# The first image's second band moves into the prelude as plain convolutions; the first batch's other work becomes one chain, one piece a turn

## The chip, the cores and the metric

The kernel runs on one core of one Trainium2 chip. The core has five engines with instruction queues of their own: TensorE (PE in the profile, its weight loads PEld), VectorE (DVE), ScalarE (ACT), GpSimd (POOL) and SyncE (SP, which here only issues transfers). Each executes its queue in the order written. The metric is the device time in microseconds; lower is better. The kernel before takes 8226.97 us, the median of 3 runs (8226.15 to 8232.14).

## The reference

The input is four images of 64 x 64 positions with 128 channels, in float32; an image is 4096 tokens. Two layers follow one another. What matters here, for each image:

```python
c1 = conv3x3(elu(x), W1) + b1              # 128 -> 128 channels
c2 = conv3x3(c1, W2) + b2                  # 128 -> 256 channels
a, b = split(c2);  c3 = a * sigmoid(b)
q, k, v = c3@Wq+bq, c3@Wk+bk, c3@Wv+bv     # 4, 4 and 16 wide, causal attention over 4096 tokens
x1 = x + c3 + tile(atten(q, k, v), 8) @ W3 + b3

y = layernorm(x1)                          # second layer
h = y + attention(y@wq, y@wk, y@wv) @ wo   # 16 heads of 8, all 4096 x 4096 scores, not causal
t = x1 + h + (silu(h@w1) * (h@w3)) @ w2
out = t + mixture(layernorm(t))            # 8 experts, the two best by a router
```

The second layer's attention is by far the largest part: 16 heads x 4096 x 4096 exponentials for each image.

## The kernel before, in words

**Units.** An image is cut into 8 *chunks* of 512 tokens (8 image rows) and into 4 *bands* of two chunks (16 rows). Bands 0 and 1 hold the chunks 0 to 3, bands 2 and 3 the chunks 4 to 7. A batch is one image.

**The main stream.** `stream` walks through a written plan of *segments*: for one image, one group of four heads and one chunk of queries, a range of key tiles of 128. Each key tile is one *step* (`attention_step`): four score matmuls into two PSUM tiles, two exponentials of 128 x 1024 on ACT, four value matmuls into `acc`. There are 1024 steps per image. Steps are written so that a step's values follow the scores of the two steps after it (`finish(2)`). Keys lie in `kx`, which has four places of a quarter of the tokens; `key_quarter` brings them, ahead of time where the segment that needs them is ready. A segment is ready when `second` of its image, the number of chunks whose second-layer operands are written, has reached `n`. For the first image the plan has three parts, with n = 2, 4 and 8: 64 steps over the first two chunks, 192 more when there are four, 768 more when there are eight. For later images n is 8.

**Other work as pieces.** Everything else is written as Python generators that yield after each *piece* (some 0.46 us of TensorE work). The list `fillers` holds them; after each step the main loop may call `insert`, which takes one piece from the first filler. While an image's operands are incomplete, the credit for this grows by 1.0 a step. If the stream isn't ready, every turn of the loop takes a piece and no step.

**The chain of one image.** `convolutions` makes ELU, layer 1 and layer 2 band by band. Most bands use the Winograd form (`winograd`): POOL builds `row_terms` and `col_terms`, TensorE does 16 products, and DVE combines them. `first_attention` makes chunk c's query, key and value terms, puts the causal steps (`first_step`, c + 1 of them) into the stream and gathers the result in `ready`. `second_operands` then folds W3, makes the layer norm, transposes, makes the second layer's queries, keys and values of a chunk and stores them to HBM (`d_q`, `d_k`, `d_v`), from where the steps load them.

**The prelude.** For the first image nothing is there to stream at the start. `run_alone` turns through five generators: the convolutions, the first attention, the second layer's operands (`second_operands_beside`), and two that transform the weights for Winograd (`fold_and_spread`, `spread_beside`). Band 0 is made by `first_band` as plain convolutions: its inner function `nine` adds nine products of 128 x 512 in one PSUM bank, for layer 1 and for each half of layer 2. The prelude ends when two chunks are complete and the three weight transforms are done; what is left of the generators goes into one filler, `together`, which takes pieces from them in turn. Until four chunks are complete, the main loop takes two pieces a turn. Later images have no `together`: their `first_attention` draws on its `convolutions` and calls `second_operands` itself, one chain.

**One order for each engine.** `InOrder` records every instruction as depending on the one before it on its engine, so a queue is exactly in the order written; every instruction carries the line of that helper, L105, and the profile is read by tile names: `s` and `e` are scores and exponentials, `qx`, `kx`, `vg` the attention's operands, `m` the PSUM bank of the pieces (one buffer), `e_band` and `c_band` the padded bands before layer 1 and layer 2 (two each), `taps` the untransformed weights (`r` holds the third set).

Of the kernel before, what the change touches and what calls it, by code (L numbers as in the profile page):

```python
# [9 lines left out]
FP = mybir.dt.float32  # L10
FR = mybir.dt.float32r
AF = mybir.ActivationFunctionType
ALU = mybir.AluOpType
AX = mybir.AxisListType

P = 128
C = 128
IMG = 64
N = IMG * IMG
NT = N // P  # L20
QB = 512
# [94 lines left out]
def fast_path(ctx: ExitStack, tc: tile.TileContext, a: dict, where: dict, out: bass.AP, verdict):  # L116
# [33 lines left out]
    def chunk(tag, name=None):  # L150
        return wk.tile([P, QB], FP, tag=tag, bufs=CHUNKS.get(tag, 1), name=name or tag)
# [8 lines left out]
    alone = [True]  # L160
# [34 lines left out]
    taps1 = taps(a["L0_conv_W1"])  # L195
# [106 lines left out]
    def rows(ap):  # L302
        return ap.rearrange("p (h w) -> p h w", w=IMG)
# [34 lines left out]
    def row_terms(band):  # L338
        r = row_tile().rearrange("p (i y x) -> p i y x", i=4, y=8)
        for i, (x, y, op) in enumerate(SUMS):  # L340
            pool.tensor_tensor(r[:, i], band[:, x : x + 15 : 2, :], band[:, y : y + 15 : 2, :], op)
        return r
# [51 lines left out]
            late.pop(0)()  # L394
            yield 0.0, "free" if late else "stop"

    def first_band(st):


        def nine(taps, band, y, n):  # L400
            ps = rows(m_tile()[:, : n * IMG])
            for m in range(9):
                i, j = divmod(m, 3)
                pe.matmul(
                    ps,
                    lhsT=taps[:, i, j, :],
                    rhs=band[:, y + i : y + i + n, j : j + IMG],
                    start=m == 0,
                    stop=m == 8,
                )  # L410
                if m in (2, 5):
                    yield 0.0, "stop"
            return ps

        pool.memset(e_band[0][:, 0, :], 0.0)
        pool.memset(c_band[0][:, 0, :], 0.0)
        for band, y, n, to in (
            (e_band[0], 0, 8, slice(1, 9)),
            (e_band[0], 8, 8, slice(9, 17)),
            (e_band[1], 0, 1, slice(17, 18)),  # L420
        ):
            ps = yield from nine(taps1, band, y, n)
            act.activation(c_band[0][:, to, 1 : IMG + 1], ps, AF.Identity, bias=b1)
            yield 0.0, "stop"
        st.c3 = wk.tile([P, 2 * QB], FP, tag="c3", bufs=2, name="c3")
        for h in range(2):
            c3, gate = st.c3[:, h * QB : (h + 1) * QB], chunk("sd", "gate")
            ps = yield from nine(taps2a, c_band[0], 8 * h, 8)
            act.activation(rows(c3), ps, AF.Identity, bias=half_b2a, scale=0.5)
            yield 0.0, "stop"  # L430
            ps = yield from nine(taps2b, c_band[0], 8 * h, 8)
            act.activation(rows(gate), ps, AF.Tanh, bias=half_b2[:, 1:2], scale=0.5)
            dve.scalar_tensor_tensor(c3, gate, 1.0, c3, ALU.add, ALU.mult)
            st.done.append(c3)
            yield 0.0, "stop"

    def tiles(ap):

# [2 lines left out]
    def convolutions(b, st):  # L441
# [75 lines left out]
        jobs = [(0, 0), (0, 1), (0, 2), (1, 0), (0, 3), (1, 1), (1, 2), (1, 3)]  # L517
        yield from elu(3)
        if b == 0:
            yield from first_band(st)  # L520
            jobs = [(0, 1), (0, 2), (1, 1), (0, 3), (1, 2), (1, 3)]
            while len(spread_of) < 3:
                yield 0.0, "wait"
            yield from elu(5)
        else:
            pool.memset(e_band[0][:, 0, :], 0.0)
        r_ = row_terms(e_band[jobs[0][1]])
        v = [col_terms(r_, j) for j in COLS]
        yield 0.0, "stop"
        for n, (layer, r) in enumerate(jobs):  # L530
            ahead, terms = [], []
            at_once = False
            if n + 1 < len(jobs):
                layer_, r_next = jobs[n + 1]
                if layer_ == 0:
                    yield from elu(min(2 * r_next + 3, NQ))
                    if r_next == 3:
                        pool.memset(e_band[1][:, 17, :], 0.0)

                at_once = layer_ == 0 or layer == 1 or r_next + 1 < r  # L540
                if at_once:
                    terms.append(row_terms((c_band if layer_ else e_band)[r_next % 2]))

            def used(q):
                if at_once:
                    ahead.append(col_terms(terms[0], COLS[q]))

            if layer == 0:
                yield from winograd(wino1, slice(0, C), v, b1, used, first(r))
                here, above = c_band[r % 2], c_band[(r - 1) % 2]  # L550
                if r == 0:
                    pool.memset(here[:, 0, :], 0.0)
                else:
                    pool.tensor_copy(here[:, 0, :], above[:, 16, :])
                    pool.tensor_copy(above[:, 17, :], here[:, 1, :])
                if r == 3:
                    pool.memset(here[:, 17, :], 0.0)
            else:
                while b == 0 and len(st.ready) < 2 * r - 2:
                    yield 0.0, "wait"  # L560
                st.c3 = wk.tile([P, 2 * QB], FP, tag="c3", bufs=2, name="c3")
                yield from winograd(wino2, slice(0, C), v, half_b2a, lambda q: None, second(r, False))
                yield from winograd(wino2, slice(C, 2 * C), v, b2[:, 1:2], used, second(r, True))
                st.done += [st.c3[:, :QB], st.c3[:, QB:]]
                yield 0.0, "done"
            if n + 1 < len(jobs) and not at_once:
                terms.append(row_terms(c_band[r_next % 2]))
                ahead = [col_terms(terms[0], j) for j in COLS]
            v = ahead
# [8 lines left out]
    def first_attention(b, st):  # L578
# [3 lines left out]
        for c in range(NQ):  # L582
            while len(st.done) <= c:

                r = (0.0, "wait") if b == 0 else next(st.conv)
                if r[1] != "done":
                    yield r
            while b == 0 and st.second < c - 1:
                yield 0.0, "wait"
            c3 = st.done[c]  # L590
            t = xt
# [46 lines left out]
            dve.tensor_tensor(t, ps, t, ALU.add)  # L638
            yield 0.6, "stop"

            while b == 0 and st.read < c:
                yield 0.0, "wait"
            sums, found = [], []
            for r in range(c + 1):
# [1 line left out]
            while not found:  # L646
                yield 0.0, "rounds"
            st.ready.append((t, found[0]))
            while b > 0 and st.second <= c:
                yield from second_operands(b, st)  # L650
        dve.tensor_reduce(seen[:, 0, b : b + 1], top0.rearrange("p i c -> p (i c)"), AX.X, ALU.max)
        dve.tensor_reduce(seen[:, 1, b : b + 1], top_v0, AX.X, ALU.max)
# [87 lines left out]
    def second_operands_beside(b, st):  # L740

        while st.second < NQ:
            while len(st.ready) <= st.second or not folded[0]:
                yield 0.0, "wait"
            yield from second_operands(b, st)

# [293 lines left out]
    class Batch:  # L1040


        def __init__(self, b):

            dims = {
                "t": [NQ, P, QB],
                "h": [NQ, P, QB],
                "k": [P, 2, N],
                "q": [NQ, P, 2, 2, QB],
                "v": [NG1, P, NQ, 4 * NSLOT * (1 + HD1)],  # L1050
                "a": [NQ, NG1, P, QB],
                "r": [NQ, P, QB // HD1],
                "g": [NQ, P, P],
            }
            if b == 0:
                dims["p"] = [NG1, NQ, P, QB]
            self.d = {name: dram.tile(shape, FP, tag=name, name="d_" + name) for name, shape in dims.items()}
            self.done, self.ready, self.second, self.read = [], [], 0, 0
            self.conv = convolutions(b, self)
            scratch.append(self.d)  # L1060
            batches.append(self)

    batches = []

    def together(gens):

        gens = list(gens)
        while gens:
            for _ in range(len(gens)):
                r = next(gens[0], None)  # L1070
                while r is not None and r[1] in ("held", "rounds"):
                    yield r
                    r = next(gens[0], None)
                gen = gens.pop(0)
                if r is not None:
                    gens.append(gen)
                    if r[0] > 0.0:
                        yield r[0], "stop"
                        break
                if not gens:  # L1080
                    return
            else:
                yield 0.0, "stop"

    def run_alone(gens, until):

# [181 lines left out]
    def spread_beside():  # L1268
# [4 lines left out]
    st = batches[0]  # L1273
    left = run_alone(
        [st.conv, first_attention(0, st), second_operands_beside(0, st), fold_and_spread(), spread_beside()],
        lambda: st.second >= plan[0].n and len(spread_of) == 3,
    )
    alone[0] = False
    fillers.append([together(left), PREPARE, None, False])

    steps = stream()
    credit, waiting = 0.0, False
# [4 lines left out]
    while True:  # L1287
# [22 lines left out]
        free = bool(fillers) and fillers[0][3]  # L1310
        if waiting or not quiet[0] and (free or credit > 0.0 and (left >= PIECE or credit > 2.8)):
            took = insert()
            if b == 0 and batches[0].second < plan[0].n + 2:
                took += insert()
            credit -= took
            left -= took
        ahead = min(max(left, 0.0), AHEAD)
# [721 lines left out]
```

## Time and profile before

| | |
|---|---|
| median of 3 runs | 8226.97 us |
| profiled execution | 8229.92 us |
| its span in the trace | 8228.1 us |
| granted TensorE clock, mean | 0.988 |
| ACT busy, share of the span | 7866.6 us, 96% |
| PE busy, share of the span | 8022.1 us, 97% |
| DVE and POOL busy | 2459.5 and 681.1 us |
| exponentials of 128 x 1024 and their busy time | 8480, 7809.3 us |

The execution's time beside its span is what lies around the trace's first and last instruction. Busy time is counted once where instructions of one engine overlap, so one exponential takes 7809.3 / 8480 = 0.92 us of ACT, a step 1.84, although its own duration is given as 1112 ns. A window view gives the busy time of each engine between two moments, with the granted clock of TensorE. In a timeline the brackets name the idle time before an instruction and what ended it.

### The profile page before, as it was taken

How to read it: one execution, taken by the hardware profiler on the slowest of the kernel's cores; microseconds unless marked ns; L12 is line 12 of the kernel's file. 1: busy time of each engine (PE TensorE's matmuls, PEld its weight loads, DVE VectorE, ACT ScalarE, POOL GpSimd, SP SyncE). 2: the span in 40 equal slices, each digit the busy share in tenths (PEclk: the TensorE clock that was granted, in tenths of full speed). 3: DMA queues.
4: the chain of work that ended last, by engine and by line, in shares of the span. 5: the costliest groups of instructions: out<-in, count | busy, mean ns of one | idle time of the engine just before them, and what ended most of it. 6: DMA issues, size and time to landing. Idle time of an engine off the chain costs nothing.

```text
span 8228.1 us, 173041 instructions
## 1 busy us (share of the span) xinstructions
PE 8022.1 (97%) x73335; PEld 2481.8 (30%) x73335; DVE 2459.5 (30%) x5068; ACT 7866.6 (96%) x8679; POOL 681.1 (8%) x615
## 2 busy tenths in 40 slices
PE   6799999999999999999999999999999999999998
PEld 3222222222333332333333333222333333232233
DVE  5433122222332222333332223333333332121123
ACT  2499999999999999999999999999999999999996
POOL 3201101000000012110000002211000000000000
PEclk8899999999999999999999999999999999999999
DMA  2122010101110100011110000001111111111121
GB/s 70 52 67 76 24 42 30 51 27 45 49 34 17 39 22 26 34 38 49 38 36 24 27 27 28 28 30 48 35 48 45 47 47 52 37 37 42 58 68 33
DMA packets 213940, 334.24 MB, mean 41 GB/s; under 512 B 31555, under 2 KB 107811, under 8 KB 213155
## 3 DMA queue, kind: packets, MB, share of 16 engines
q1 hardware_dynamic: 209139, 321.31, 12.0%
q8 instruction: 577, 9.45, 0.5%
q10 hardware_dynamic: 4016, 1.77, 0.1%
q14 instruction: 208, 1.70, 0.1%
HBM read 195.09 MB, written 127.93 MB: 39 GB/s over the span
## 4 chain that ended last, share of the span: by engine, by line
PE 67%; issue 3%; ACT 1%; DVE 1%; POOL 0%; DMA 0%; ACTq 0%; DVEq 0%; POOLq 0%
PE acc L105 33%; PE s L105 22%; PE m L105 13%; ACT e L105 1%; DVE h L105 0%; POOL rs L105 0%; DVE added L105 0%; DVE at L105 0%; ACT neg L105 0%; POOL xt L105 0%; ACT t L105 0%; DVE by_e L105 0%; POOL v L105 0%; ACT th L105 0%; DMA d_r<-sums 0%
## 5 line engine op out<-in xcount | busy, mean ns | idle before, releaser
L105 ACT ACTIVATE e<-s 128x1024 f32<-128x1024 f32 x8480 | 7809.3, 1112 | 91.5 <-PE s L105 87.1
L105 PE MATMUL acc<-e,vg 128*9 128x512 f32 x32768 | 4333.7, 594 | 1.9 <-DVE at L105 1.9
L105 PE MATMUL s<-qx,f_kx 32*128 32x512 f32 (+1 forms) x16960 | 2909.2, 495 | 37.5 <-ACT e L105 27.7
L105 PEld LDWEIGHTS s<-qx,f_kx 32*128 32x128 f32 (+1 forms) x16960 | 1171.2, 181 | 4079.0 <-ACT e L105 3859.7
L105 PEld LDWEIGHTS acc<-e,vg 128*9 128x9 f32 x32768 | 715.9, 90 | 797.1 <-issue 463.7
L105 PE MATMUL m<-v,f_wino 128*32 128x256 f32 x5744 | 470.9, 405 | 54.9 <-DVE sd L105 16.8
L105 DVE TENSOR_TENSOR by_e<-m,gates 128x512 f32<-128x512 f32 x248 | 171.5, 691 | 736.9 <-PE m L105 733.9
L105 POOL TENSOR_TENSOR v<-r 128x1024 f32<-128x1024 f32 x120 | 232.6, 1945 | 1314.1 <-PE m L105 1313.6
L105 DVE COPY sd<-m 128x512 f32<-128x512 f32 x179 | 123.7, 691 | 673.6 <-PE m L105 673.6
L105 PE MATMUL m<-f_we,y2T 128*32 128x256 f32 x3968 | 316.9, 391 | 0.5 <-DVE by_e L105 0.5
L105 POOL TENSOR_TENSOR rs<-ve,f_minus_half 128x4 f32<-128x4 f32 x64 | 65.2, 1018 | 3029.2 <-DVE ve L105 3029.2
L105 DVE COPY at<-acc 128x512 f32<-128x512 f32 x130 | 89.9, 691 | 698.8 <-PE acc L105 696.4
L105 DVE TENSOR_REDUCE added<-by_e 128x128 f32<-128x1024 f32 x128 | 255.3, 1995 | 4.8 <-DMA d_g<-turned 0.5
L105 PE MATMUL m<-hT,f_fw 128*32 128x256 f32 (+1 forms) x2728 | 236.1, 391 | 0.0
L105 POOL TENSOR_TENSOR t<-t,h 128x512 f32<-128x512 f32 x32 | 41.0, 1281 | 2042.1 <-DVE h L105 2042.1
L105 DVE TENSOR_TENSOR t<-m,sums 128x256 f32<-128x256 f32 x135 | 57.3, 425 | 493.2 <-PE m L105 493.2
L105 PEld LDWEIGHTS m<-v,f_wino 128*32 128x32 f32 x5744 | 121.9, 111 | 247.2 <-issue 172.2
L105 DVE SCALAR_TENSOR_TENSOR h<-m,h 128x512 f32<-128x512 f32 (+1 forms) x93 | 64.2, 690 | 434.8 <-ACT th L105 276.3
L105 DVE TENSOR_TENSOR t<-m,t 128x512 f32<-128x512 f32 x62 | 42.9, 692 | 444.4 <-PE m L105 444.4
L105 DVE COPY h<-m 128x512 f32<-128x512 f32 (+1 forms) x93 | 64.2, 690 | 370.5 <-PE m L105 370.5
L105 PE MATMUL m<-e,f_v 128*32 128x512 f32 (+2 forms) x1128 | 149.7, 574 | 0.0
L105 DVE TENSOR_TENSOR e<-e,f_consts 128x128 f32<-128x128 f32 x128 | 29.1, 287 | 326.3 <-ACT e L105 326.3
(253 smaller groups left out, 3299.1 us busy)
## 6 DMA issues: line engine op xcount, KB each, us to landing
f_kx<-d_k SPq DMA_DIRECT2D x139, 512.0 KB
qx<-d_q SPq DMA_DIRECT2D x152, 256.0 KB
d_q<-two SPq DMA_DIRECT2D x64, 512.0 KB
d_a<-at SPq DMA_DIRECT2D x128, 256.0 KB
vg<-d_v SPq DMA_DIRECT2D x32, 576.0 KB
d_k<-two SPq DMA_DIRECT2D x32, 512.0 KB
d_v<-vc SPq DMA_DIRECT2D x32, 288.0 KB
xe<-in_x_dram SPq DMA_DIRECT2D x32, 256.0 KB
```

Of the source, the lines that this page charges most:

```text
L105: made = op(*args, **kw)
```

## The change

- `first_band` becomes `first_bands`: after band 0 it makes band 1 in the same way, with nine products for each bank, in the prelude. Ahead of it come the ELU pieces up to chunk 4 (the last row of layer 1 needs one row of the next band). Layer 1 is needed for the row above, which POOL copies from band 0.
- The prelude ends only when these two bands are done too (`st.plain`), beside the conditions of before.
- The Winograd jobs of the first image shrink from six to four, bands 2 and 3 in both layers, in the order (layer 1, band 2), (layer 1, band 3), (layer 2, band 2), (layer 2, band 3). Before, the order was layer 1 of bands 1 and 2, layer 2 of band 1, layer 1 of band 3, layer 2 of bands 2 and 3.
- `together` goes. After the prelude the generators become separate fillers, the second operands first, then the first attention. `second_operands_beside` returns at its first wait once the prelude is over, and the first attention then draws on the convolutions and calls `second_operands` itself. The waits of the first image that were bound to `b == 0` are bound to the prelude.
- The second piece a turn goes.

```diff
-    def first_band(st):
+    def first_bands(st, elu):
...
+        for r in range(2):
+            here, there = e_band[r], e_band[1 - r]
+            c_here = c_band[r]
+            if r == 0:
+                pool.memset(here[:, 0, :], 0.0)
+                pool.memset(c_here[:, 0, :], 0.0)
+            else:
+                yield from elu(5)
+                pool.tensor_copy(c_here[:, 0, :], c_band[0][:, 16, :])
+            for band, y, n, to in (
+                (here, 0, 8, slice(1, 9)),
+                (here, 8, 8, slice(9, 17)),
+                (there, 0, 1, slice(17, 18)),
+            ):
+                ps = yield from nine(taps1, band, y, n)
+                act.activation(c_here[:, to, 1 : IMG + 1], ps, AF.Identity, bias=b1)
+                yield 0.0, "stop"
+            st.c3 = wk.tile([P, 2 * QB], FP, tag="c3", bufs=2, name="c3")
+            for h in range(2):
...
+        st.plain = False
...
         if b == 0:
-            yield from first_band(st)
-            jobs = [(0, 1), (0, 2), (1, 1), (0, 3), (1, 2), (1, 3)]
+            yield from first_bands(st, elu)
+            jobs = [(0, 2), (0, 3), (1, 2), (1, 3)]
             while len(spread_of) < 3:
                 yield 0.0, "wait"
-            yield from elu(5)
+            yield from elu(7)
...
-                r = (0.0, "wait") if b == 0 else next(st.conv)
+                r = (0.0, "wait") if alone[0] else next(st.conv)
...
-            while b > 0 and st.second <= c:
+            while not alone[0] and st.second <= c:
                 yield from second_operands(b, st)
...
             while len(st.ready) <= st.second or not folded[0]:
+                if not alone[0]:
+                    return
                 yield 0.0, "wait"
...
-        lambda: st.second >= plan[0].n and len(spread_of) == 3,
+        lambda: st.second >= plan[0].n and len(spread_of) == 3 and not st.plain,
     )
     alone[0] = False
-    fillers.append([together(left), PREPARE, None, False])
+    fillers.extend([gen, PREPARE, None, False] for gen in reversed(left[1:]) if gen is not st.conv)
...
             took = insert()
-            if b == 0 and batches[0].second < plan[0].n + 2:
-                took += insert()
```

More of the change, by code (lines that the diff above doesn't have):

```diff
@@ L413, in nine @@
             return ps
[L415 to L435, printed above, removed]
+        for r in range(2):
[17 more added lines that the diff above has]
+            for h in range(2):
+                c3, gate = st.c3[:, h * QB : (h + 1) * QB], chunk("sd", "gate")
+                ps = yield from nine(taps2a, c_here, 8 * h, 8)
+                act.activation(rows(c3), ps, AF.Identity, bias=half_b2a, scale=0.5)
+                yield 0.0, "stop"
+                ps = yield from nine(taps2b, c_here, 8 * h, 8)
+                act.activation(rows(gate), ps, AF.Tanh, bias=half_b2[:, 1:2], scale=0.5)
+                dve.scalar_tensor_tensor(c3, gate, 1.0, c3, ALU.add, ALU.mult)
+                st.done.append(c3)
+                yield 0.0, "stop"
@@ L519, in convolutions @@
         if b == 0:
-            yield from first_band(st)
-            jobs = [(0, 1), (0, 2), (1, 1), (0, 3), (1, 2), (1, 3)]
+            yield from first_bands(st, elu)
+            jobs = [(0, 2), (0, 3), (1, 2), (1, 3)]
             while len(spread_of) < 3:
                 yield 0.0, "wait"
-            yield from elu(5)
+            yield from elu(7)
         else:
             pool.memset(e_band[0][:, 0, :], 0.0)
-        r_ = row_terms(e_band[jobs[0][1]])
+        r_ = row_terms(e_band[jobs[0][1] % 2])
         v = [col_terms(r_, j) for j in COLS]
@@ L558, in convolutions @@
             else:
-                while b == 0 and len(st.ready) < 2 * r - 2:
+                while alone[0] and len(st.ready) < 2 * r - 2:
                     yield 0.0, "wait"
@@ L583, in first_attention @@
             while len(st.done) <= c:
-                r = (0.0, "wait") if b == 0 else next(st.conv)
+                r = (0.0, "wait") if alone[0] else next(st.conv)
                 if r[1] != "done":
                     yield r
-            while b == 0 and st.second < c - 1:
+            while alone[0] and st.second < c - 1:
                 yield 0.0, "wait"
@@ L639, in first_attention @@
             yield 0.6, "stop"
-            while b == 0 and st.read < c:
+            while alone[0] and st.read < c:
                 yield 0.0, "wait"
@@ L1058, in __init__ @@
             self.done, self.ready, self.second, self.read = [], [], 0, 0
+            self.plain = b == 0
             self.conv = convolutions(b, self)
@@ L1063, in fast_path @@
     batches = []
[L1065 to L1083, printed above, removed]
     def run_alone(gens, until):
```

## The prediction

> **What bounds the kernel now.** I read the busy shares first, then a table of the span cut at the visible changes of pace. The Trainium skill ("Perfetto Trace Analysis", section "Identifying the Most-Contended Engine") says that occupancy is a fair measure for ScalarE and that busy matmul time isn't one for TensorE, so I follow ACT. The page:
>
> ```profile
> PE 8022.1 (97%) x73335; PEld 2481.8 (30%) x73335; DVE 2459.5 (30%) x5068; ACT 7866.6 (96%) x8679; POOL 681.1 (8%) x615
> ACT  2499999999999999999999999999999999999996
> ```
>
> The stages (window, its length, then busy us of each engine, PE clock, DMA share, GB/s):
>
> ```profile
> 0.00:153.50 153.50, 97.25 (x370) 48.50 (x370) 81.95 (x168) 15.57 (x22) 48.17 (x68) 0.84 0.28 82
> 153.50:326.00 172.50, 149.50 (x1479) 47.96 (x1480) 78.61 (x162) 134.49 (x145) 45.87 (x36) 0.99 0.12 35
> 326.00:412.80 86.80, 49.54 (x464) 19.23 (x464) 49.22 (x91) 0.76 (x2) 30.10 (x24) 0.55 0.23 80
> 412.80:750.00 337.20, 322.46 (x2880) 98.62 (x2880) 123.58 (x282) 319.94 (x352) 26.20 (x25) 0.96 0.23 74
> 750.00:1250.00 500.00, 496.00 (x4154) 144.59 (x4152) 120.53 (x238) 498.05 (x548) 78.58 (x63) 1.00 0.12 38
> 1250.00:8150.00 6900.00, 6867.62 (x63814) 2098.40 (x63810) 1972.85 (x4055) 6885.48 (x7600) 449.81 (x398) 1.00 0.12 38
> ```
>
> Length minus ACT busy is ACT's idle time: 137.9, 38.0, 86.0, 17.3, 1.9 and 14.5 us, then 65.8 in the tail. From 750 us on ACT never stops; the exponentials are the same number in both kernels. So the change is worth what it does to the 281.1 us of ACT idle before 1250. Stage 1 is the prelude. Stage 2 is the first 64 attention steps (142 exponentials: 128, and 14 of the first attention), stretched by two pieces a turn. Stage 3 is one wait, seen on ACT's timeline:
>
> ```profile
> 409.84 0.63 ACT L105 ACTIVATE t<-t 128x512 f32<-128x512 f32 x1 [83.71 <-DVE t L105]
> 412.85 1.02 ACT L105 ACTIVATE e<-s 128x1024 f32<-128x1024 f32 x1 [2.38 <-PE s L105]
> ```
>
> Step 65 belongs to a segment that needs chunks 2 and 3 (four ready). They come from band 1, whose Winograd convolution only starts at the end of the prelude; when the 64 steps run out, its second layer is still to do.
>
> **What the built order shows.** The instruction order of the changed program (not its time) settles what the diff leaves open. TensorE executes matmuls in program order; the skill says so ("TensorE: Matmul & The Clock Gate", section "Step-by-step: what each phase is for": only weight loads are pulled ahead), and a late operand in this trace does hold everything (7.04 us below). In the order, the second half of the key product of chunk 3 moves from the wait after step 64 to step 24; chunk 7's moves from step 199 to step 254. From step 1570 on the filler work stands where it stood.
>
> **Removed.** The 86.0 us wait at step 64 goes: chunk 3 is complete 40 steps (40 x 1.84 = 74 us) early. The double pieces of stage 2 go. A 4.9 us key-load wait inside stage 4, at the first use of the other two key places, goes too: with four chunks ready during the first segment, those places are loaded ahead.
>
> **Added: a longer prelude.** The first band shows what a plain band costs (PE timeline):
>
> ```profile
> 31.45 7.99 PE L105 MATMUL m<-f_e_band,taps 128*128 128x512 f32 x18 [0.78 <-ACT f_c_band L105]
> 40.23 2.22 PE L105 MATMUL m<-f_e_band,taps 128*128 128x64 f32 x18 [0.78 <-ACT f_c_band L105]
> 42.90 7.96 PE L105 MATMUL m<-f_c_band,taps 128*128 128x512 f32 x18 [0.45 <-issue]
> ```
>
> A nine takes some 7.8 us, and about 1 us to the next one for ACT to empty the bank. Following the new order:
> - Up to 88.6 (transposes of chunk 1) nothing moves. Then band 1's ELU pieces enter ahead of chunk 1's first attention. The vector queue (query terms, layer norm of chunk 0, key terms, ELU) lets the scores start about 99 instead of 90.3; chunk 1's sums are copied about 106.5 instead of 101.4. Band 1's first nine starts about 108.
> - First layer: 2 x 7.8 + 2.2 + 3 gaps of 1 = 21; pieces between: value and key products 1.24 + 1.03, W3 fold 2 x 0.6, one transpose 0.66. About 25, to 133.
> - Second layer: 4 x 7.8 + 4 gaps = 35; pieces between: wq1 1.1, values 1.24, keys 1.03, wq0 1.1 with its 1.3 wait, wk0/wv0 0.6, transpose 0.6, fold 0.6, three first steps 3 x (0.5 + 1.8) with 2.4 for ACT to free score banks. About 51, to 184.
> - Tail: the stream's first score stands behind chunk 3's query and key terms and chunk 2's layer norm on DVE (2.7 + 1.0 + 1.9 + 1.9 + 1.4 with POOL's power + 1.1), transposes 0.7, copy 0.9, half a product 0.6: 13 with latencies, to 197.
> - Clock: the skill (same page, section "Part 1: The HAM clock gate") puts the array at half rate until about 3.4 us of sustained work. The trace agrees: the first nine of all took 10.13 against 7.99. I add 2 there and 4 in the thin parts: **first exponential at 203**, 49.5 later.
>
> ACT busy within the prelude becomes 15.6 + 7 evacuations (4.5) + 6 exponentials moved here (5.6) = 25.7; idle 177.3, against 137.9: **+39.4**. The Winograd terms that POOL built there (about 19 us) go; they were off this path. The first key load has no late writer in front of it any more.
>
> **Steps 1 to 256.** One piece a turn. In stage 4, which already ran so, idle other than the 4.9 and 3.8 us DMA waits was 8.6 in 337 us; 2.5% of about 530 us (286 steps with the first attention's 30, at 1.84) is 13. To this: 3 for the start. 4 because one chain has no second piece to lie between dependent ones. At step 80 layer 2 of band 2 follows layer 1 of band 3 in the same chain, and POOL makes its row terms and first column term between; before, the other chain covered that place, but its like in the stall shows the price:
>
> ```profile
> 331.83 4.69 POOL L105 TENSOR_TENSOR r<-f_c_band 128x528 f32<-128x528 f32 x4
> 338.57 1.93 PE L105 MATMUL m<-v,f_wino 128*32 128x256 f32 x16 [7.04 <-POOL v L105]
> ```
>
> 7 less about 1 of scores in stock: 6. Nothing on PE can pass it, the next scores and values wait behind it.
>
> At step 257 comes the other cost: the segment needs all eight chunks; chunk 7's last product is issued in step 254, and the key load can't be issued before its write. The pair of transfers at the end of the old wait (SP, then PE):
>
> ```profile
> 403.36 0.54 SPq L105 DMA_DIRECT2D d_k<-two  x1
> 406.80 0.54 SPq L105 DMA_DIRECT2D f_kx<-d_k  x1
> 411.95 0.80 PE L105 MATMUL s<-qx,f_kx 32*128 32x512 f32 x4
> ```
>
> 8.6 us. After step 254's scores: product 0.95, DVE 2.0, transfers 8.6 = 11.6; three steps cover 5.5: **6**. The second batch's image loads stand ahead of the keys on SP (0.8 us each to issue), so up to 10. They replace the 3.8 wait that those loads caused in ACT's queue at 726 us. Sum for steps 1 to 256: 13 + 3 + 4 + 6 + 6 = **32**; and 6 for the rest to 1250 (1.9 before, with the second batch's preparation squeezed into 768 steps instead of 825).
>
> **Sum.** Idle 281.1 before; after 177.3 + 32 + 6 = 215.3: 65.8 less. ACT's work grows by 4.5 - 1.9 (one copy, two tanh) = 2.6. So 63 us less: span 8228.1 - 63 = 8165, execution 8167 (it read 8229.92). The median of the runs lies 3 us below that execution: **8164**, -0.77%.
>
> **Rivals.**
> - *Better, about 8138 (0.12).* The prelude ends at 192 as counted without a cold clock (-11), and steps 1 to 256 lose only 17 (-15). For it: band 0's nines kept clock 1.00 with the same gaps.
> - *A late step 257, 8184 (0.13).* Key load, values, queries and the second batch's image loads leave together, and one-chain waits cost 10 more: +20. For it: that prelude load took 11.3 us from the vector engine's last write to the first score. Against: little else moves then (74 GB/s in stage 4).
> - *Cold prelude, about 8206 (0.08).* At the 0.57 to 0.64 clock that the old prelude shows from 100 to 150, the 54 wide matmuls (46 us) take some 42 more. Against: old PE was idle half of that time; now it is nearly packed. At 0.55 in the old wait there were gaps behind every 1.9 us piece, here behind 8 us.
> - *Slower, about 8247 (0.04).* Removing the alternation of chains makes each piece wait on DVE for the one before it, and in-order PE passes the wait to ACT. The order has 170 turns with a piece in steps 1 to 256, of which I charge 17 us (0.10 each). It decides from (17 + 63)/170 = 0.47 us each; at stage 2's 38.0 / 64 = 0.59, 100 us, and 20 us over the old time. Against: between two pieces lie scores and values (about 1.4 us), more than the 0.7 copy that frees the bank; later batches run one chain with hardly any idle, though at lower density.
> - *The change doesn't take hold (0.02).* Step 65 still waits as long: 8164 + 86 = 8250. Only transfers 40 steps late could bring it; the order speaks against it.
>
> **Numbers.** The likeliest has 0.61, by itself 8150 to 8180. Range 8138 to 8204: it takes in the better case, the late step and nearly the cold one. A measurement of this kernel can tell about 0.2% (16 us). Faster needs below 8210.5: 0.61 + 0.12 + 0.13 + 0.06 of the cold case = 0.92; within 0.2% lies the rest of that, 0.02; slower are the last two, 0.06.
>
> **What would show it.** First exponential of the stream at 198 to 208. No ACT gap over 10 us after it. Step 64 done about 130 us after it (68 steps with the first attention's four). One gap near step 80, ended on POOL's column terms, and one of 4 to 10 us near 765, ended by keys. ACT idle to the end of step 256 near 210. Wrong if the prelude runs past 225, or if small PE waits on DVE add up to over 60 us in steps 1 to 256.

## The result, and the profile after

The changed kernel takes 8155.07 us (median; 8154.1 to 8159.66), beside 8229.15 us for the kernel before in the same session: 74 us less, ratio 0.9911, 95% interval 0.9894 to 0.9928. Forecast were 8164 us and a range of 8138 to 8204.

The page of the changed kernel, the two lines that answer to those shown of before:

```profile
PE 7997.1 (98%) x73041; PEld 2477.0 (30%) x73041; DVE 2415.5 (30%) x5001; ACT 7866.4 (96%) x8683; POOL 646.2 (8%) x592
ACT  1899999999999999999999999999999999999996
```

ACT does the same work as before (7866.4 against 7866.6 us) in a span of 8153.2 instead of 8228.1, so the 74.9 us between the spans are, but for 0.2, ACT's idle time. The windows of the changed kernel, cut at its own changes of pace (window, length, then busy us of PE, weight loads, DVE, ACT and POOL, clock, DMA share, GB/s):

```profile
0.00:190.95 190.95, 140.71 (x522) 67.91 (x526) 82.79 (x201) 23.52 (x34) 27.86 (x57) 0.95 0.24 70
190.95:330.00 139.05, 127.49 (x1148) 38.61 (x1152) 51.05 (x96) 124.95 (x137) 30.01 (x23) 0.94 0.25 84
330.00:740.00 410.00, 401.36 (x3752) 123.20 (x3748) 147.59 (x323) 400.97 (x441) 48.06 (x42) 0.99 0.18 59
740.00:768.00 28.00, 17.15 (x116) 4.47 (x108) 6.02 (x17) 17.90 (x22) 2.08 (x2) 0.82 0.53 170
768.00:1250.00 482.00, 478.01 (x4050) 140.15 (x4052) 124.74 (x242) 479.08 (x527) 85.76 (x68) 1.00 0.12 37
```

Length minus ACT busy: 167.4 us idle in the prelude, then 14.1, 9.0, 10.1 and 2.9. Together 203.6, where the kernel before had 281.1 in the stages that these replace; the rest of the span has 3 us more. The prelude ends 37.4 us later (first exponential at 190.95 instead of 153.51) with 29.5 us more idle time, the 83.71 us wait is gone, and the stream runs from 191 us on with five gaps of more than 1.7 us up to step 257. ACT's timeline of the changed kernel (in brackets the idle time ahead and what ended it):

```profile
231.06 20.30 ACT L105 ACTIVATE e<-s 128x1024 f32<-128x1024 f32 x22 [1.79 <-PE s L105]
...
266.13 1.94 ACT L105 ACTIVATE e<-s 128x1024 f32<-128x1024 f32 x2 [4.41 <-PE s L105]
...
301.45 1.94 ACT L105 ACTIVATE e<-s 128x1024 f32<-128x1024 f32 x2 [4.45 <-PE s L105]
...
366.10 59.28 ACT L105 ACTIVATE e<-s 128x1024 f32<-128x1024 f32 x64 [8.77 <-PE s L105]
...
751.32 1.94 ACT L105 ACTIVATE e<-s 128x1024 f32<-128x1024 f32 x2 [9.44 <-PE s L105]
```

PE's waits in 190.95 to 768 us say what it waited for there (total, times, longest):

```profile
PE s L105 <- DMA f_kx<-d_k: 19.4, 3, 9.8
PE m L105 <- POOL v L105: 7.3, 1, 7.3
PE s L105 <- issue: 1.8, 1, 1.8
```

Three of the gaps are key loads (two of 4.4 and the one at step 257), one is POOL building Winograd terms (366 us), and the one at 231 us has no releaser named here (`issue`). TensorE's waits of pieces for DVE, which the slower rival rested on, come to under 1 us in all.

### The profile page after: what moved, and what is told of

It reads as the page before. It is cut to its first block, busy times and chain, and to the rows that moved or that the text cites. A ratio compares the mean times of both kernels' runs of the same rounds, so it can differ in the third digit from the quotient of the medians.

```text
span 8153.2 us, 172350 instructions
## 1 busy us (share of the span) xinstructions
PE 7997.1 (98%) x73041; PEld 2477.0 (30%) x73041; DVE 2415.5 (30%) x5001; ACT 7866.4 (96%) x8683; POOL 646.2 (8%) x592
## 4 chain that ended last, share of the span: by engine, by line
PE 90%; issue 6%; ACT 2%; DVE 1%; DMA 1%; POOL 1%; SPq 0%; ACTq 0%; POOLq 0%; DVEq 0%
PE acc L105 43%; PE s L105 29%; PE m L105 18%; ACT e L105 1%; DVE h L105 0%; DMA f_kx<-d_k 0%; POOL rs L105 0%; DVE at L105 0%; POOL xt L105 0%; ACT t L105 0%; DMA xe<-in_x_dram 0%; SPq L105 0%; ACT neg L105 0%; DVE added L105 0%; DMA taps<-in_L_conv_W_dram 0%
## 5 line engine op out<-in xcount | busy, mean ns | idle before, releaser
L105 ACT ACTIVATE e<-s 128x1024 f32<-128x1024 f32 x8480 | 7807.1, 1110 | 81.7 <-PE s L105 75.9
L105 PE MATMUL m<-v,f_wino 128*32 128x256 f32 x5376 | 429.9, 391 | 7.3 <-POOL v L105 7.3
L105 PE MATMUL m<-e,f_v 128*32 128x512 f32 (+1 forms) x1104 | 146.5, 574 | 0.0
```

Source lines behind the costliest of these rows:

```text
L105: made = op(*args, **kw)
```

## The experiments

Times are compared with the kernel before in the same session: 8227.23 us for the first four, 8228.34 for the next four, 8233.7 for the last two. The intervals of the ratios are about 0.0017 (14 us) to each side, so where two kernels lie closer than that, their times don't separate them, and the text goes by the gaps in their traces (one profiled execution each).

**The three parts of the change, apart.** The change has a plain second band (A), one chain in place of the alternation (B) and one piece a turn in place of two (C).

A alone: the changed kernel with `together`, its waits bound to the first image, and the second piece put back.

```diff
-    fillers.extend([gen, PREPARE, None, False] for gen in reversed(left[1:]) if gen is not st.conv)
+    fillers.append([together(left), PREPARE, None, False])
...
             took = insert()
+            if b == 0 and batches[0].second < plan[0].n + 2:
+                took += insert()
```

> The changed kernel with the alternation of chains and the second piece a turn put back: the plain second band alone. Theory: the plain band in the prelude brings all of the gain (the 86 us wait at step 64 against some 40 us of prelude), and the single chain brings nothing but two new gaps (8.8 us on POOL's terms at step 80, 9.4 us on the keys at step 257, where alternation has chunk 7 done at step 212): 8140, so 15 faster than the changed kernel. Rival: the single chain and single pieces carry a good part of the gain (stage 2's 38 us of ACT idle came from them): 8175 or more.

Measured: 8183.01 us, ratio 0.9947 (0.993 to 0.9964). The theory fell, the rival stands. The plain band alone brings 44 of the 74 us. The gap that ends on POOL's terms isn't new with the single chain either: this trace has it too, at 322 us with 8.88 us.

B and C alone: the kernel before's bands and jobs, with the changed kernel's chain and single pieces.

```diff
-        for r in range(2):
+        for r in range(1):
...
-            jobs = [(0, 2), (0, 3), (1, 2), (1, 3)]
+            jobs = [(0, 1), (0, 2), (1, 1), (0, 3), (1, 2), (1, 3)]
...
-            yield from elu(7)
+            yield from elu(5)
```

> The kernel before with one chain and one piece a turn, second band still Winograd after the prelude. Theory: the work after the prelude is the same, so the wait at step 64 grows by about what the 64 steps gain: ACT idle of the 64 steps 38 down to about 15, wait 86 up to about 105, and the new gap at step 257: 8235, no faster than before. Rival: the single chain is worth 20 us or more by itself: 8210 or less.

Measured: 8200.62 us, ratio 0.9967 (0.9954 to 0.9979), 27 us faster than before. The rival was right (8210 or less). I had expected the wait at step 64 to grow by what the 64 steps gained. The windows of this kernel (prelude, the 64 steps, the wait) show that it hardly did:

```profile
0.00:149.69 149.69, 92.53 (x340) 47.00 (x344) 80.36 (x164) 15.58 (x23) 44.29 (x65) 0.84 0.29 84
149.69:272.58 122.89, 121.92 (x1144) 36.42 (x1144) 42.58 (x73) 118.57 (x129) 34.61 (x27) 0.96 0.14 44
272.58:382.00 109.42, 67.40 (x544) 24.87 (x536) 57.67 (x130) 19.01 (x23) 15.24 (x13) 0.55 0.19 66
```

Idle of ACT: 4.3 us in the 64 steps (38.0 before), 90.4 in the wait (86.0 before). In the wait ACT also does 19 us of causal steps that lay in the 64 steps before. So the second piece a turn, together with the alternation, had cost 34 us of ACT time and had shortened the wait by only some 4. Which of the two did it this run can't tell, since it takes both out. Beside the changed kernel (8155) it gives the plain band's worth once more: some 46 us.

A and B, two pieces a turn, with the second `insert` as in the first diff:

> The changed kernel with two pieces a turn until four chunks are complete. Theory: chunk 3 is complete at step 12 instead of 23 and chunk 7 at step 246 instead of 253, which takes most of the 9.4 us gap at step 257 (-8); the dozen doubled turns cost 0.6 each and some (+8): 8155, within 6 us of the changed kernel. Rival: double pieces cost what stage 2 before suggested, 1.4 us a turn and all the rest: 8170.

Measured: 8168.44 us, ratio 0.9928 (0.9911 to 0.9944): the rival's value. Dropping the second piece is worth some 13 us to the chain, although two pieces bring chunk 3 to its end in half the steps (its keys are stored in step 11 instead of 24, 15 us earlier). The intervals overlap, but the traces agree: in the first 70 us of the stream ACT works 55.3 us here and 66.3 us in the changed kernel.

A and C, alternation with one piece a turn, the first diff without its last two lines:

> The changed kernel with alternation put back but one piece a turn. Theory: chunk 3 is complete at step 40, chunk 7 at step 235, so neither gap (POOL's terms at step 80, keys at step 257) is left: 8140, like the plain band alone. Rival: the waits behind late keys at the first group changes stay or grow since chunk 3's stores now lie later in SP's queue: 8155 or more.

Measured: 8144.01 us, ratio 0.9897 (0.988 to 0.9913). That is 39 us less than A alone, from the second piece only. Of the theory half held: step 257 has no gap any more, but the one on POOL's terms stays, with 8.66 us at 344. The pair shows where the 39 us were lost. ACT's timeline of the kernel with A alone, while pieces go in twos:

```profile
229.09 1.94 ACT L105 ACTIVATE e<-s 128x1024 f32<-128x1024 f32 x2 [1.23 <-PE s L105]
232.81 1.94 ACT L105 ACTIVATE e<-s 128x1024 f32<-128x1024 f32 x2 [1.78 <-PE s L105]
236.41 1.94 ACT L105 ACTIVATE e<-s 128x1024 f32<-128x1024 f32 x2 [1.66 <-PE s L105]
```

and its TensorE there:

```profile
232.21 0.51 PE L105 MATMUL s<-qx,f_kx 32*128 32x512 f32 x4
232.65 0.64 PE L105 MATMUL m<-v,f_wino 128*32 128x256 f32 x8
234.38 0.64 PE L105 MATMUL m<-v,f_wino 128*32 128x256 f32 x8 [1.09 <-DVE t L105]
234.81 1.07 PE L105 MATMUL acc<-e,vg 128*9 128x512 f32 x8
235.80 0.50 PE L105 MATMUL s<-qx,f_kx 32*128 32x512 f32 x4
```

The pieces share one PSUM bank. The second piece of a turn stands directly behind the first, so it waits 1.09 us for DVE to empty the bank, and a turn takes 3.59 us where ACT needs 1.84. The wait is only part of it: without it the turn would still take 2.50 us, because two pieces are more than fits beside a step's scores and values. TensorE in the kernel with A and C:

```profile
229.48 0.64 PE L105 MATMUL m<-v,f_wino 128*32 128x256 f32 x8
229.94 1.04 PE L105 MATMUL acc<-e,vg 128*9 128x512 f32 x8
230.91 0.51 PE L105 MATMUL s<-qx,f_kx 32*128 32x512 f32 x4
231.34 0.64 PE L105 MATMUL m<-v,f_wino 128*32 128x256 f32 x8
```

Here a turn takes 1.86 us, about what ACT needs: scores and values lie between two pieces and cover the emptying, and TensorE's time is just enough. The windows of the first 70 us of the stream, of A alone and then of A and C:

```profile
193.48:262.90 69.42, 54.00 (x508) 19.25 (x506) 35.34 (x73) 38.12 (x41) 28.05 (x22) 0.80 0.22 77
```

```profile
193.37:262.90 69.53, 65.77 (x584) 20.73 (x582) 29.03 (x61) 60.20 (x66) 25.10 (x20) 0.88 0.25 84
```

ACT does 22 us more work in the same time; 11 of the rest come up to 770 us (479.5 against 490.3 us of ACT work). In the first 70 us TensorE's waits of pieces for DVE are 14.4 us with A alone and 2.8 with A and C. The other 10 us are left to the second pieces' own time and to the lower clock (0.80 against 0.88), which these runs don't separate. A kernel with two PSUM banks for the pieces, which would take the wait out and leave the second piece in, was not run.

So of the 74 us, about 44 are the plain band's, and the other 30 come with the chain and the single piece together. How these divide depends on what stands beside them. The single piece is worth 39 us to the alternation and 13 to the chain; the chain changes the time by -15 with two pieces (8183 to 8168) and by +11 with one (8144 to 8155), and its two intervals overlap each time. The single piece alone, without the band and with the alternation, was not run. The trace of A and C does show the 9.44 us gap at step 257 gone, because chunk 7's keys are stored in step 235 instead of 253.

**The gaps that remain.** Keys ahead: the changed kernel, with each quarter of keys loaded as soon as its place is free of all segments in between and its chunks are written.

```diff
+        def keys_ahead(at, kt):
+            seg = plan[at]
+            taken = {seg.place(q) for q in range((kt + 1) // 8, seg.hi // 8)}
+            for later in plan[at + 1 : at + 13]:
+                for q in range(later.lo // 8, later.hi // 8):
+                    if later.place(q) in taken:
+                        continue
+                    taken.add(later.place(q))
+                    if len(batches) > later.b and batches[later.b].second >= min(later.n, 2 * q + 2):
+                        key_quarter(later, q)
...
-                if kt % 8 == 7:
-                    for later in plan[at + 1 :]:
...
+                keys_ahead(at, kt)
```

> The changed kernel, but keys are loaded as soon as their place and their chunks are free and written, not at the end of the last segment that used the place or at the segment's start. Theory: the gaps of 1.8, 4.4 and 4.5 us at the changes of head group and most of the 9.4 us at step 257 are key loads that stand on SP behind late stores of chunk 3 and chunk 7: 8155 - 11 - 6 = 8138. Rival: the loads only change places with queries and values, which arrive later by as much: 8150 or more.

Measured: 8137.37 us, ratio 0.9887 (0.987 to 0.9903); 8138 was expected. Of PE's waits in the same window, the longest two; no key load is left by name:

```profile
PE m L105 <- POOL v L105: 7.3, 1, 7.3
PE s L105 <- issue: 5.0, 1, 5.0
```

The gaps at 231, 266 and 301 us are gone, the one at step 257 went from 9.44 to 4.64 (the 5.0 us of `issue` above; its key load leaves only at 731.05 us, after chunk 7's store at 727.22). My reason was half wrong, though. It fits the gap at 231 us, whose key load left at 225.86 right behind a store. It does not fit the next two. SP's timeline of the changed kernel around the gap at 266:

```profile
259.04 1.20 SPq L105 DMA_DIRECT2D f_kx<-d_k  x2
260.30 0.58 SPq L105 DMA_DIRECT2D qx<-d_q  x1
```

Two key loads leave together. In the written order, the first one refills the place that the group just ended had used, for segments of the second part of the plan; it waits for that group's last scores. The second is the next group's own. Before, the second part wasn't ready during the first, that refill wasn't written, and the next group's keys left 12 us ahead of their use (174.68 us). So, by the order written and the moment at which both leave, the load that came too early in SP's queue held the one that was due.

Turns without a piece at the layer change: 

```diff
                 ahead = [col_terms(terms[0], j) for j in COLS]
+                for _ in range(5 if b == 0 else 0):
+                    yield 0.0, "free"
```

> The changed kernel with five turns without a piece where layer 2 of band 2 follows layer 1 of band 3, so that steps run while POOL makes its terms. Theory: the 8.8 us gap near 366 us is the in-order PE waiting for POOL with a piece, so it goes; but the chain ends at step 256 instead of 253, and the gap at step 257 grows by about as much: 8155, between 8150 and 8160. Rival: the gap isn't POOL's doing but stays: 8163.

Measured: 8165.1 us, ratio 0.992 (0.9904 to 0.9937), 10 us slower than expected. The gap near 366 us and PE's wait on POOL's `v` vanish, so that wait was the in-order PE with a piece whose terms weren't made. But the chain now ends at step 256, and the gap at step 257 becomes 20.41 us instead of 9.44, more than the turns gained. The same with keys ahead:

> The changed kernel with keys ahead and the five turns. Theory: -8.8 and -11 and the gap at step 257 stays near 9 since chunk 7 ends at step 256: 8137. Rival: keys ahead also covers it, since only queries and values are still to come: 8130.

Measured: 8149.12 us, ratio 0.9902 (0.9886 to 0.9919). Neither value held; ACT's timeline shows why:

```profile
738.39 0.63 ACT L105 ACTIVATE neg<-xe 128x512 f32<-128x512 f32 x1 [18.48 <-DMA xe<-in_x_dram]
```

Chunk 7 is done too late, and the next image has begun: its ELU stands in ACT's queue, its transposes in PE's, ahead of the first score, and both wait for an image load. To see how much of the 18.5 us is the image, its first ELU piece was put twelve turns after its loads:

```diff
-        yield 0.0, "stop"
+        for _ in range(12 if b > 0 else 1):
+            yield 0.0, "stop"
```

> The chain with keys ahead and five turns (8149), and the next image's first ELU piece twelve turns after its loads are issued. Theory: at step 257 the gap of 18.5 us is chunk 7's own end (keys and queries of a chunk that is done a step too late, some 12 us) and behind it ACT and PE held by pieces that wait for the image's load (6 us); the second part goes: 8142. Rival: the gap is all chunk 7's, nothing changes: 8149.

Measured: 8142.15 us, ratio 0.9888 (0.9871 to 0.9904), the expected value. The 7 us between the two medians are within what the intervals can't separate; the traces give the image's pieces about 5 us (gaps of 18.48 and 2.10 us before, one of 15.71 now). The rest is chunk 7's: PE now waits 10.8 us for its queries (`qx<-d_q`).

**Best version.** Alternation with one piece a turn, keys ahead and the five turns, first without and then with the image's pieces later:

> Alternation of chains and one piece a turn (8144 by itself), with keys ahead and the five turns. The chain ends at step 243, so nothing is paid at step 257. Theory: 8144 - 8.7 (POOL's terms) - 4.6 (keys) = 8131. Rival: gaps move to other pieces that wait on the layer norm (9.4 us on PE for DVE xt): 8140 or more.

Measured: 8138.64 us, ratio 0.9887 (0.9871 to 0.9904). Neither clearly: 5 of the 13 us came, which the intervals don't separate from none. The key gap and the POOL gap are gone, but 5.3 us at 206 us (pieces on DVE at the start) and 3.77 us for the image's load stand, and smaller ones near 574 us.

> Alternation, one piece a turn, keys ahead, five turns (8138.6), and the next image's first ELU piece twelve turns after its loads. Theory: the 3.8 us that ACT waits for the image's load goes: 8135. Rival: the pieces that start twelve turns later run closer to their end at step 1024 and cost as much again: 8139 or more.

Measured: 8133.6 us against 8233.7, ratio 0.9879 (0.9863 to 0.9896), the fastest kernel of this study, 1.2% under the kernel before. Against the changed kernel (0.9911) the intervals still touch; what supports the gain is that its trace has no gap of ACT over 4 us from the start of the stream to the last 70 us of the program, where gaps of 21 and 14 us stand in every kernel. The 3.77 us for the image's load are gone, and the late image pieces cost nothing that can be seen.

## Why the prediction was right, and where its terms were off

- **The wait at step 64.** Right: 86.0 us of idle gone, chunk 3's keys stored in step 24, as the order on the engines had told.
- **The prelude.** The mechanism is right, the size off: 177.3 us idle forecast, 167.4 measured, and the first exponential came at 191 instead of 203, outside the 198 to 208 given as a sign. Two terms were too large. Of the 6 us for a low clock about 1 was paid: the clock was 1.00 from 107 to 176 us, and the first nine of band 1 ran at full rate from its start (2.74 us for three products, as later), TensorE having worked without a gap for 5 us before it; only the thin end (clock 0.80 from 176 to 191) took 14 us where 13 were counted without the allowance. And the two layers took 23 and 46 us instead of 25 and 51. ACT's extra work came to nothing in the total (2.6 us forecast, -0.2 measured), since its exponentials took 2.2 us less (7807.1 against 7809.3).
- **Steps 1 to 256.** 32 us forecast, 33.2 measured, but the parts don't agree, and that the sum agrees is luck. POOL's terms cost 8.8 instead of 6 and step 257 cost 9.4 instead of 6. The text laid POOL's gap on the single chain; the traces of A alone and of A and C, which alternate, have it as well. The general loss was taken at 13 + 4, and is some 3: a piece every turn costs the chain next to nothing. In its place came 10.7 us of key loads at the group changes, which I had not seen: I counted the earlier readiness of the second part only as a gain (the 4.9 us wait in stage 4, which did go).
- **The second piece a turn.** The sum counts its removal rightly, within stage 2's 38.0 us of idle, but the text put it beside the plain band as if the band carried the gain. The experiments show that its removal alone is worth 39 us beside the alternation and 13 beside the chain, so it can carry as much of the 74 us as the 30 that the band leaves; and that, together with the chain, it pays without the band as well (27 us).
- **Rivals.** The better case hit the prelude (192; measured 191), but not by its reason alone: counted without a cold clock, the prediction's own terms end at 197, and the other 6 us are mostly the shorter layers. Its second half, 17 us for the steps, did not come (33.2). The late step 257 came at 9.4 us, near the top of the 10 that the forecast allowed, not at 20 more. The cold prelude is refuted by the clock; its sum was off too, since 46 us at 0.57 to 0.64 take 26 to 35 more, not 42. The slower case is refuted for the single chain: PE waited under 1 us for DVE over all pieces, where 0.47 us on each of 170 would have been needed. What it describes is part of what two pieces a turn did. That the change doesn't take hold is refuted by the wait that is gone.
- **From 768 us on.** Up to 1250 us 2.9 us of idle against the 6 forecast; after that nothing moved, as forecast, but for 3 us more.

## What to carry to other kernels

Before putting more side work into a turn, count what the turn holds on each engine: one piece just fitted here (1.86 us of TensorE against ACT's 1.84), a second did not, even without its wait. And two pieces that share one buffer should not stand next to each other in the queue of an engine that also feeds the bottleneck: work of the main stream between them hides the emptying. The second piece brought chunk 3's end 15 to 20 us nearer (the chain, the alternation) and cost 11 to 22 us of ACT time meanwhile; it paid in neither case. Before loading something early, look at what the load waits for: in an in-order queue of transfers, a prefetch that waits for its place holds the load that is due (twice 4.4 us here). And if a chain of side work has a deadline, its end a few steps ahead can be worth more than the gaps that one closes inside it: the five turns closed a gap of 8.8 us and lost some 10 us in all, or 12 with keys ahead.

## What was unexpected of the hardware

- TensorE's clock stayed low while its bursts were short. In the old wait it fell during the 7.04 us wait for POOL's terms and was then granted at 0.50 from 340 to 412.8 us, although TensorE was busy for 44.3 of these 72.8 us, mostly in bursts of 1.9 us with gaps of 0.8 to 3.4 us; over the wait of the second experiment the mean was 0.55 again. The nines of the changed kernel's prelude, most of them with pieces between and gaps of up to 1.6 us, kept 1.00 from 107 to 176 us. Side work that filled the wait thus ran at half rate for most of it. This may be part of why the wait for the second band was 86 us there, and the prelude only 37 us longer here; no run tested it.
